# Sums of probabilities for the softmax denominator: two of four heads go from VectorE to GpSimd

## The chip, the cores and the metric

The kernel runs on one core of a Trainium2 chip. The metric is the device time of one launch in microseconds (us). A core has five engines that run their own queues in order and wait for each other by semaphores: TensorE (PE, matmuls), VectorE (DVE), ScalarE (ACT), GpSimd (POOL) and SyncE (SP, which here issues all later DMAs).

## The reference

The input has 8 sequences of 1024 rows and 512 columns. One transformer layer is computed in float32: layer norm, attention with 16 heads from latent projections and rotary embedding, a residual, layer norm, a gated FFN whose operands are rounded blockwise to an FP4 grid, a residual.

```python
scores = jnp.einsum('bhqd,bhkd->bhqk', Q, K)
scores = jnp.clip(scores, -80.0, 80.0)
scores = jnp.where(causal, scores, -jnp.inf)
weights = jax.nn.softmax(scores / jnp.sqrt(jnp.float32(d_qk)), axis=-1)
attn = jnp.einsum('bhqk,bhkd->bhqd', weights, V)
...
gate = fp4_linear(x, w_gate)
y = fp4_linear(x, w_up)
h = jax.nn.silu(gate) * y
return fp4_linear(h, w_down)
```

The change touches the softmax's denominator: the sum of the probabilities over all keys, for each query and head.

## The kernel before

The work is cut into 16 units `u` of 512 rows, two to a sequence. Attention of a unit runs over 4 groups `hq` of four heads, and in a group over blocks `j` of 128 keys: 3 steps in an even unit (the first half of a sequence, whose last step takes two narrow blocks), 7 in an odd one. That makes 320 steps. Scores are computed with the keys on the partitions, so a probability tile `pT` is 128 keys x 4 heads x 512 queries, and the denominator is a sum over partitions and over steps.

One step (`score_step`, from L589 on): TensorE computes the scores of the four heads into the one score bank `sc_ps`; ScalarE takes the exp in two halves of two heads each into `pT` (L629); VectorE clips the first half (L645), GpSimd clips the second (L648). In masked steps GpSimd also zeroes the triangle, first of the second half, then of the first (L653). `weigh`, the second part of a step, is put off until the scores of the next step are issued (`flush(1)`): TensorE multiplies `pT` with the values into the bank `num`.

The denominator has two ways. In units 1 and 3 TensorE multiplies every `pT` with ones. In all others ("summed") the first `pT` of a group is kept as accumulator, and VectorE adds each later `pT` to it (L680), two heads an instruction; a last step has four adds, of two widths. After a group's last step `divide` lets TensorE multiply the accumulator with ones (bank `den`), and `normalise` turns, inverts and multiplies on VectorE (L737 to L740).

`pT` has three buffers. One holds the accumulator until `divide`, which runs in step 1 of the next group, and the weights `wo` of the output projection take one for a while; the others alternate. An exp can therefore start only when the `pT` of two steps before is released by its readers and adders.

Between the steps TensorE's queue is filled with other pieces: the next unit's projections, the output projection (`out_proj`, L814 on VectorE), and the FFN of rows finished earlier: `gate` (copied out by ScalarE, L141, silu L893), `up` (multiplied on VectorE from PSUM, L907), `down` (L943). In units 0 to 3 the weights are quantised in place of the FFN. Three PSUM banks `ps_t` serve all these pieces. VectorE rounds the activations to the FP4 grid in chains of short instructions on the tiles `h`, `y`, `wraw` and `m` (L226 to L280). Small statistics of the layer norm run on GpSimd (L346 to L352), and ScalarE applies them (L360).

The order of every engine's queue is fixed when the program is built. A planner (`Clock`) keeps an estimated time for each of TensorE, VectorE and ScalarE. VectorE's instructions are of two kinds: urgent ones go through `on_dve(cost, ready, run)`, which first lays spare instructions that fit before `ready`; spare ones wait in two lists (`slack`) with a cost and a time from which they may run. The adds of L680 are spare ones of the first list; `need(key)` lays what is left of them before a buffer is reused or a sum is read. GpSimd is not planned.

## Time and profile before

| what | value |
|---|---|
| median of 3 runs | 3518.63 us (3517.95 to 3518.91) |
| the profiled execution's own time | 3518.86 us |
| its span, first to last instruction | 3517.1 us |
| ScalarE, exp of a half tile (L629) | 640 instructions, 566.3 us |
| GpSimd, clip (L648) | 320 instructions, 337.7 us |
| GpSimd, masks (L653) | 384 instructions, 231.3 us |
| VectorE, clip (L645) | 320 instructions, 229.3 us |

A profile is one execution. Busy times are unions of an engine's instructions; a wait is the idle time of an engine just before an instruction, put down to the instruction that ended it. A group of instructions is told as line, engine, operation, tiles written and read, shapes, count, then busy time and mean length in ns, then the idle time before them. In waits, the engine and line that waited stands first, then who was waited for. The timeline gives start, length, engine, line and operation.

### The profile page before, as it was taken

How to read it: one execution, taken by the hardware profiler on the slowest of the kernel's cores; microseconds unless marked ns; L12 is line 12 of the kernel's file. 1: busy time of each engine (PE TensorE's matmuls, PEld its weight loads, DVE VectorE, ACT ScalarE, POOL GpSimd, SP SyncE). 2: the span in 40 equal slices, each digit the busy share in tenths (PEclk: the TensorE clock that was granted, in tenths of full speed). 3: DMA queues.
4: the chain of work that ended last, by engine and by line, in shares of the span. 5: the costliest groups of instructions: out<-in, count | busy, mean ns of one | idle time of the engine just before them, and what ended most of it. 6: DMA issues, size and time to landing. Idle time of an engine off the chain costs nothing. (4 is left out here: it accounts for less than half of the span.)

```text
span 3517.1 us, 101866 instructions
## 1 busy us (share of the span) xinstructions
PE 3440.5 (98%) x45428; PEld 1526.8 (43%) x45428; DVE 2923.4 (83%) x5308; ACT 1326.2 (38%) x1850; POOL 769.0 (22%) x1086
## 2 busy tenths in 40 slices
PE   8999999999999999999999999999999999999999
PEld 3333344444444444444444444444444444444444
DVE  6878759789977889887989778899778988699887
ACT  4444443434333343333343333434343333333211
POOL 3333322112121221221221212212212222111100
PEclk9999999999999999999999999999999999999999
DMA  3212111111021101121110211111211111100110
GB/s 98 70 49 71 47 36 52 50 36 30 20 64 32 55 26 32 35 59 50 32 32 20 67 29 54 30 32 32 61 49 32 32 32 49 50 20 20 56 32 17
DMA packets 190066, 148.46 MB, mean 42 GB/s; under 512 B 126524, under 2 KB 128060, under 8 KB 189628
## 3 DMA queue, kind: packets, MB, share of 16 engines
q1 hardware_dynamic: 187780, 141.09, 13.5%
q8 instruction: 356, 5.83, 0.7%
q10 hardware_dynamic: 1848, 0.87, 0.1%
q14 instruction: 82, 0.67, 0.1%
HBM read 94.72 MB, written 33.55 MB: 36 GB/s over the span
## 5 line engine op out<-in xcount | busy, mean ns | idle before, releaser
L629 ACT ACTIVATE pT<-sc_ps 128x1024 f32<-128x1024 f32 (+1 forms) x640 | 566.3, 937 | 1069.4 <-PE sc_ps L122 835.8
L648 POOL TENSOR_SCALAR pT<-pT 128x1024 f32<-128x1024 f32 (+1 forms) x320 | 337.7, 1055 | 2325.4 <-ACT pT L629 2247.0
L122 PE MATMUL pg<-yT,wu_T 128*32 128x256 f32 x11264 | 638.5, 380 | 0.0
L122 PE MATMUL pg<-yT,wg_T 128*32 128x256 f32 x11264 | 634.5, 379 | 1.7 <-ACT yT L859 0.8
L122 PE MATMUL pd<-wd_T,h 128*32 128x512 f32 x5632 | 616.8, 592 | 2.9 <-DVE h L236 2.9
L122 PEld LDWEIGHTS pg<-yT,wg_T 128*32 128x32 f32 x11264 | 366.2, 110 | 276.9 <-issue 37.2
L680 DVE TENSOR_TENSOR pT<-pT 128x1024 f32<-128x1024 f32 (+3 forms) x528 | 459.8, 898 | 25.3 <-POOL pT L653 21.7
L122 PEld LDWEIGHTS pg<-yT,wu_T 128*32 128x32 f32 x11264 | 360.0, 110 | 264.6 <-issue 33.5
L645 DVE TENSOR_SCALAR pT<-pT 128x1024 f32<-128x1024 f32 (+1 forms) x320 | 229.3, 716 | 195.8 <-ACT pT L629 194.7
L122 PEld LDWEIGHTS pd<-wd_T,h 128*32 128x32 f32 x5632 | 182.3, 110 | 415.8 <-issue 389.8
L122 PE MATMUL sc_ps<-qc,kT 32*128 32x512 f32 (+3 forms) x3072 | 338.3, 525 | 10.8 <-ACT pT L629 10.8
L141 ACT COPY h<-pg 128x512 f32<-128x512 f32 x192 | 105.5, 550 | 629.6 <-PE pg L122 629.6
L122 PE MATMUL num<-pT,v 128*32 128x512 f32 (+3 forms) x3072 | 314.0, 496 | 17.4 <-POOL pT L653 16.9
L122 PE MATMUL sc_ps<-qr,kr 32*128 32x512 f32 (+3 forms) x3072 | 306.3, 483 | 6.9 <-DVE qr L564 6.7
L280 DVE TENSOR_TENSOR h<-h,m 128x512 f32<-128x512 f32 (+1 forms) x384 | 259.6, 676 | 10.1
L236 DVE STREAM_TRANSPOSE h<-h 128x512 f32<-128x512 f32 (+1 forms) x384 | 249.9, 658 | 4.9
L653 POOL TENSOR_SCALAR_AFFINE_SELECT pT<-pT 128x256 f32<-128x256 f32 (+1 forms) x384 | 231.3, 622 | 25.2 <-DVE pT L645 10.7
L122 PE MATMUL po<-wo,aT 128*32 128x512 f32 x2048 | 225.1, 596 | 9.1 <-DMA wo<-in_w_o_dram 4.5
L907 DVE TENSOR_TENSOR h<-pg,h 128x512 f32<-128x512 f32 x192 | 122.9, 640 | 118.5 <-PE pg L122 110.6
L122 PEld LDWEIGHTS sc_ps<-qc,kT 32*128 32x128 f32 x3072 | 114.3, 183 | 208.7 <-issue 149.8
L122 PEld LDWEIGHTS sc_ps<-qr,kr 32*128 32x128 f32 x3072 | 144.0, 185 | 114.1 <-issue 77.8
L122 PEld LDWEIGHTS num<-pT,v 128*32 128x32 f32 x3072 | 64.5, 108 | 220.8 <-issue 119.0
(97 smaller groups left out, 3528.5 us busy)
## 6 DMA issues: line engine op xcount, KB each, us to landing
xo<-in_x_dram SPq DMA_DIRECT2D x64, 256.0 KB, 2.7
wo<-in_w_o_dram SPq DMA_DIRECT2D x16, 1024.0 KB, 5.2
mid<-xo SPq DMA_DIRECT2D x64, 256.0 KB, 2.8
y<-mid SPq DMA_DIRECT2D x64, 256.0 KB, 2.8
xr<-mid SPq DMA_DIRECT2D x64, 256.0 KB, 2.7
out_dram<-xr SPq DMA_DIRECT2D x64, 256.0 KB, 2.0
xp<-in_x_dram SPq DMA_DIRECT2D x30, 512.0 KB, 3.8
xnT<-xp SPq DMA_DIRECT2D x416, 32.0 KB, 2.0
```

The lines of the kernel that those rows point to most:

```text
L122: nc.tensor.matmul(dst, **kw)
L141: on_act(0.1 + 0.0009 * src.free_size(), lambda: nc.scalar.copy(dst, src))
L236: 0.06 + 0.0013 * part.shape[1], lambda: nc.vector.transpose(part, part), key
L280: nc.vector.tensor_tensor(part, part, got["m"], op)
L629: lambda: nc.scalar.activation(part, sc[:, 2 * k : 2 * k + 2, :cols], AF.Exp, scale=SM_SCALE),
L645: lambda: nc.vector.tensor_scalar(part, part, E_HI, E_LO, ALU.min, ALU.max),
L648: nc.gpsimd.tensor_scalar(part, part, E_HI, E_LO, ALU.min, ALU.max)
L653: nc.gpsimd.affine_select(out=diag, in_=diag, pattern=[[0, 2], [0, len(segs)], [1, P]], compare_op=ALU.is_ge, fill=0.0, base=0, channel_mu ...
L680: lambda a=whole, b=part: nc.vector.tensor_tensor(a, a, b, ALU.add),
L907: lambda: nc.vector.tensor_tensor(h, pg, h, ALU.mult),
```

## The change

GpSimd adds up the probabilities of heads 2 and 3 of a group, the half that it clips itself; VectorE adds only heads 0 and 1. GpSimd's adds are issued in `weigh`, so in GpSimd's queue they stand behind the next step's clip and masks. One instruction covers two heads, as before. The planner gets a time for GpSimd (`pool`) with costs for the clip, the masks and the adds, and a table `summed` of the times at which GpSimd's adds are over; a reused `pT` and the sum of `divide` wait for them in the plan. The time `ready`, from which a step's spare adds and `weigh` are planned, is now taken from the planned ends of VectorE's and GpSimd's work.

```diff
     class Clock:
-        pe = dve = act = silu = 0.0
+        pe = dve = act = pool = silu = 0.0
         shape = None
         soon, later = deque(), deque()
-        done = {}
+        done, summed = {}, {}
...
+    def on_pool(cost, ready, run):
+        clk.pool = max(clk.pool, ready) + cost
+        run()
...
             clk.need(old, pe=False)
-            clk.act = max(clk.act, clk.done.get(old, 0.0))
+            clk.act = max(clk.act, clk.done.get(old, 0.0), clk.summed.get(old, 0.0))
             del live[old]
...
             else:
-                nc.gpsimd.tensor_scalar(part, part, E_HI, E_LO, ALU.min, ALU.max)
+                on_pool(
+                    0.08 + 0.00096 * wide,
+                    ready + 0.2,
+                    lambda: nc.gpsimd.tensor_scalar(part, part, E_HI, E_LO, ALU.min, ALU.max),
+                )
...
         while masks:
-            masks.pop()()
-        ready = clk.act + 0.4 + 0.0009 * wide + (0.7 if masked else 0.0)
+            on_pool(0.5 if len(segs) == 1 else 0.72, clk.dve, masks.pop())
+        ready = max(clk.dve, clk.pool) + 0.2
...
-            for half in halves:
+            for half in halves[:1]:
                 for _, off, at in segs:
                     whole, part = acc[0][:, half, off:], pT[:, half, at : at + U - off]
...
+            for _, off, at in segs if summed and j > 0 else ():
+                whole, part = acc[0][:, 2:4, off:], pT[:, 2:4, at : at + U - off]
+                on_pool(
+                    0.1 + 0.0044 * (U - off),
+                    ready,
+                    lambda: nc.gpsimd.tensor_tensor(whole, whole, part, ALU.add),
+                )
+                clk.summed[key] = clk.summed["sum", u, hq, 0] = clk.pool + 0.2
             live[key] = j > 0 or not summed
...
         def divide():
             clk.need(key)
+            clk.pe = max(clk.pe, clk.summed["sum", u, hq, 0])
             den = bank("den")
```

## The prediction

> **What bounds the kernel now.** I read the page first, then TensorE's waits for all 3517 us and for the part after 440 us, then VectorE and GpSimd by shape, then the timeline, and last the order of instructions that the changed source builds.

> From the page of the kernel before:

> ```profile
> span 3517.1 us, 101866 instructions
> PE 3440.5 (98%) x45428; PEld 1526.8 (43%) x45428; DVE 2923.4 (83%) x5308; ACT 1326.2 (38%) x1850; POOL 769.0 (22%) x1086
> L680 DVE TENSOR_TENSOR pT<-pT 128x1024 f32<-128x1024 f32 (+3 forms) x528 | 459.8, 898 | 25.3 <-POOL pT L653 21.7
> ```

> TensorE (PE) is busy for 3440.5 us of 3517.1; about 77 us is everything that a change to other engines can give back, 2.2%. VectorE (DVE) is the second engine with 83%, GpSimd (POOL) has 78% free. The third line is the work that the change splits: 528 adds, 459.8 us.

> TensorE's waits after 440 us (columns: total us, times, longest):

> ```profile
> PE sc_ps L122 <- ACT pT L629: 6.1, 9, 1.1
> PE num L122 <- POOL pT L653: 5.9, 10, 1.1
> PE sc_ps L122 <- DVE qr L564: 5.0, 6, 1.4
> PE pv L122 <- DVE h L907: 4.8, 3, 1.6
> PE pf L122 <- ACT kT L141: 3.9, 3, 1.3
> PE pd L122 <- DVE h L236: 2.9, 4, 0.9
> ```

> The list is short and its numbers small. All rows of this view released by VectorE or GpSimd sum to 22.3 us in 30 waits; the same sum for the first 440 us is 20.6 us in 20 waits (without the 6.3 us at the very start). So even a VectorE that is never late gives back at most 43 us. The adds themselves are nearly absent from TensorE's waits: the relief lies on an engine that is mostly not waited for.

> **What the change does to the order.** In the program built from the changed source TensorE's and ScalarE's instructions stand in the same order, one for one; SP differs in three swaps of neighbouring DMAs. VectorE has 264 adds fewer and its queue is reordered, GpSimd has 264 adds more. Each stands behind the next step's clip and masks (L648, L653), so no mask of the next step waits for it. The adds wait for GpSimd's own earlier work, which stands ahead anyway; three of them name TensorE too, whose reading is long past. New is one wait: an exp (L629) writes a probability tile that now also has to be released by GpSimd's add.

> **VectorE's side, removed.** By shape, the 528 adds are 192 of 1024 columns at 1219 ns, and 112 each of 768, 512 and 256 at 962, 733 and 451 ns. Half of each goes: 96 x 1.219 + 56 x (0.962 + 0.733 + 0.451) = 237 us.

> **GpSimd's side, added.** The trace has no wide two-input add on GpSimd. The nearest row is its clip of the same tile, one input: those clips that no VectorE instruction overlaps took 1.04 us for 1024 columns and 0.83 for 768, so 0.84 ns a column over a fixed 0.18, which gives 0.61 for 512 and 0.40 for 256. Lower end for an add of 1024 columns: 1.04 us, the second input free. Upper end: two clips and a wait for a whole VectorE add of 1.22, 3.3 us. I take two clips, 2.08 us, since a second operand of the same size is read (1.65, 1.22 and 0.80 for the narrower ones). Sum: 96 x 2.08 + 56 x (1.65 + 1.22 + 0.80) = 405 us; between 203 and 728 at the ends. GpSimd would go from 769 to some 1240 us with its own delays: it is free for that.

> **What the add does to VectorE.** This decides. Two places in the timeline:

> ```profile
> 226.12 1.04 POOL L648 TENSOR_SCALAR pT<-pT 128x1024 f32<-128x1024 f32 x1 [3.19 <-ACT pT L629]
> 226.41 1.30 DVE L645 TENSOR_SCALAR pT<-pT 128x1024 f32<-128x1024 f32 x1
> ...
> 232.08 1.29 POOL L648 TENSOR_SCALAR pT<-pT 128x1024 f32<-128x1024 f32 x1 [4.91 <-DVE wraw L266]
> ...
> 232.51 1.14 DVE L277 TENSOR_SCALAR m<-m 128x512 f32<-128x512 f32 x1
> ```

> VectorE's clip starts inside GpSimd's and ends at 227.71, 0.55 us after GpSimd ends at 227.16; undisturbed it takes 0.69. The step on `m` takes 1.14 us in place of 0.43. Over the whole trace, against the median of undisturbed instructions of the same line and shape, VectorE loses 153 us and GpSimd 148 us in this way. Stretched are VectorE's instructions with two SBUF inputs and its tensor_scalars; transposes, reductions and those that read PSUM keep their time (L907: 685 ns alone, 683 overlapped). So the two engines hold each other up, and a longer GpSimd instruction holds VectorE longer. GpSimd's present work is 629 us undisturbed: VectorE loses 0.24 us for each us of it. That is the low end for the adds, since the clip often runs while VectorE is between tasks. The adds start just where VectorE is not: in the 2 us behind the masks VectorE is busy 95% of the time, 72% with the kinds that are held. High end 0.72. I take 0.55, nearer to the high end as it is measured in the very place. 405 us of adds then cost VectorE 223 us (97 to 292) against 237 saved: **net 14 us less, between 140 less and 55 more**. The offload is about a draw on the engine that it is to relieve.

> [...]

> **The new wait of the exp.** For each summed step I took from the trace the room between the end of GpSimd's masks of the next step and the start of the exp after it, in which the add must fit. The median is 7.8 us, the least -1.5; 30 of 206 rooms are too small, by 42 us in all. What stands behind the late exp on ScalarE is the copies of PSUM banks, and TensorE's next scores, which need the score bank. TensorE's next scores came 5 to 14 us after that exp's end in most of these places (FFN matmuls lie between), so it is hidden there; not in units 0 and 2, where steps follow each other within 5 us. Room and cover together leave 2.8 us on TensorE, 5.3 with adds stretched by a quarter (as masks and clips are, 1.10 to 1.38 times), 9.2 by 1.6. I take 5 us. If the FFN cover were gone, the whole 42 us would show.

> **The reordered queue.** The planner lets VectorE run spare work up to the moment at which it thinks that a PSUM reader or a clip is ready. It knows the adds' time on GpSimd (0.1 + 0.0044 us a column of one head) but not that they hold VectorE, so the freed time is filled by FFN quantisation and the urgent instruction is late by what the adds took. Adds run 405 of 3517 us, 12%; an urgent instruction that falls into one waits half of 2.08 us on average: 0.12 us on each of the 50 waits above, 6 us; up to 25 us if the lag stays until the next idle moment (0.5 us each).

> ScalarE's normalisation (L360) waits 92 us for GpSimd's small statistics now, in 25 waits; these queue behind adds too. By the same 0.12 us it is 3 us on ScalarE, hidden behind 62% idle time; I count nothing. GpSimd issues no DMA here.

> **Sum.** Made against the profiled execution's own 3518.9 us (span 3517.1 and 1.8 around it; the median of the runs is 3518.6): +5 (exp) +6 (late VectorE) and 0 for the relief: 3529.

> **Rivals.**
> *No change that shows*, 3519 within 7 us (0.2%, about what a measurement of this kernel can tell). Speaks for it: TensorE's order is untouched and 98% busy, VectorE's balance is a draw. Both small terms need only be half as large.
> *Faster*: the adds hold VectorE by only 0.24, VectorE ends 140 us lighter (79% busy), and half of the 43 us of its and GpSimd's lateness goes: 3519 - 21 = 3498. Against it: the planner spends the freed time on spare work, so the same urgent instructions see the same queue.
> *VectorE becomes the bound* in the odd units, at 3545 to 3586. From 700 to 900 us it is busy 180 of 200 us, so about 6 us are free for each group of four heads (60 us). There the adds sum to 4 x 2.08 + 1.65 + 1.22 + 0.80 = 12.0 us; at 0.72 they hold VectorE 8.6 us against 7.0 saved. From a sum of 18 us on (0.72 x 18 - 7 = 6), so with adds of 3.1 us and more, the free 6 us are used up. At the upper end the sum is 20.5 us, 1.8 us over in each of 24 groups: 42 us, and with the urgent instructions' 25 us it is 3586.
> That the adds don't move is excluded by the built order.

> **How the numbers follow.** Slower by 7 to 40 us: 0.38 (the forecast), VectorE the bound: 0.08, no change: 0.32, faster: 0.22. Range 3504 to 3560: it leaves out about half of the faster case below and of the bound above, and keeps the ends of the unknown costs otherwise.

> **What would show it.** GpSimd's add of 1024 columns at about 2.1 us (mean 2.3 with delays), VectorE's busy time near 2910 us in place of some 2690, VectorE's instructions on `m` and `h` longer in the mean, TensorE idle some 11 us more, most of it before 440 us at scores and `num`. Wrong would be VectorE at 2750 or less with shorter rows of waits (faster), or a VectorE above 2980 with TensorE waiting for L907 and L236 (bound).

## The result, and the profile after

The changed kernel takes 3757.5 us in the median of 4 runs (3754.3 to 3758.5), the kernel before 3518.8 (also of 4). The ratio is 1.0671, with a 95% interval of 1.0658 to 1.0684: 239 us slower. The prediction of 3529 had the sign and missed the size; its range ended at 3560.

The page of the changed kernel:

```profile
span 3755.5 us, 101919 instructions
PE 3512.3 (94%) x45428; PEld 1549.7 (41%) x45428; DVE 2983.5 (79%) x5044; ACT 1325.1 (35%) x1850; POOL 1205.2 (32%) x1350
L719 POOL TENSOR_TENSOR pT<-pT 128x1024 f32<-128x1024 f32 (+3 forms) x264 | 470.6, 1782 | 10.4
L688 DVE TENSOR_TENSOR pT<-pT 128x1024 f32<-128x1024 f32 (+3 forms) x264 | 294.4, 1115 | 18.6 <-POOL pT L661 16.8
```

VectorE has 264 adds fewer and is busy 60 us longer. TensorE does the same instructions in the same order, is busy 72 us longer and idle 167 us longer (239.5 against 72.9). So two things have to be explained, the idle time and the busy time.

The idle time, in TensorE's waits of the changed kernel (total us, times, longest):

```profile
PE po L122 <- DMA wo<-in_w_o_dram: 48.5, 14, 7.0
PE num L122 <- POOL pT L661: 38.6, 31, 3.4
PE sc_ps L122 <- DVE qr L568: 30.8, 13, 3.3
PE pg L122 <- DVE xr L960: 25.7, 5, 6.8
PE sc_ps L122 <- ACT pT L633: 16.1, 26, 1.7
PE pp L122 <- DVE xr L960: 13.7, 5, 3.3
PE pg L122 <- DVE h L924: 12.3, 7, 3.4
```

The first row was small before, and `xr` as a releaser is nearly new (0.2 us before). From the same view of the kernel before:

```profile
PE po L122 <- DMA wo<-in_w_o_dram: 4.5, 4, 2.3
```

All rows of this view, summed by the releaser:

| TensorE waits for | before, us | after, us |
|---|---|---|
| the load of `wo` and other DMAs | 6 | 48 |
| GpSimd | 17 | 39 |
| VectorE | 32 | 129 |
| ScalarE | 17 | 23 |

The busy time is, nearly all of it, the clock. The mean granted clock of the two profiles:

```profile
core 0: 3517.1 us, clock 0.999
core 0: 3755.5 us, clock 0.977
```

Behind the mean stand stretches in which TensorE is granted half its clock: 3 within the span before, 35 after. Half their length, "the clock's loss" below, is 4.0 us before and 85.3 after. Part of it falls into TensorE's idle time. While TensorE is busy the stretches last 6.4 us before and 140.2 after; half of that is 3.2 and 70.1 us, so 67 of the 72 us of busy time are the clock's. 167 us of idle time and 72 of busy time are the 238 us by which the span grew (rounded).

VectorE is held up as the prediction described. By the same count, the length of its instructions against the median of undisturbed ones of the same kind, it loses 431 us to GpSimd, 153 before. Of the two kinds shown, the step on `m` is one that the prediction saw stretched, and it is longer in the mean; the transpose was not stretched, and it is not longer. After (the figure behind the busy time is the mean in ns):

```profile
L281 DVE TENSOR_SCALAR m<-m 128x512 f32<-128x512 f32 x254 | 165.0, 650 | 8.7
L240 DVE STREAM_TRANSPOSE h<-h 128x512 f32<-128x512 f32 x320 | 222.8, 701 | 3.8
```

and before:

```profile
L277 DVE TENSOR_SCALAR m<-m 128x512 f32<-128x512 f32 x254 | 122.0, 480 | 8.7
L236 DVE STREAM_TRANSPOSE h<-h 128x512 f32<-128x512 f32 x320 | 222.8, 702 | 4.1
```

The late load of `wo`, in the timeline of the changed kernel:

```profile
2099.39 0.83 POOL L655 TENSOR_SCALAR pT<-pT 128x768 f32<-128x768 f32 x1 [3.51 <-ACT pT L633]
...
2100.30 1.29 POOL L661 TENSOR_SCALAR_AFFINE_SELECT pT<-pT 128x512 f32<-128x512 f32 x2
...
2101.56 2.28 POOL L719 TENSOR_TENSOR pT<-pT 128x768 f32<-128x768 f32 x1
...
2102.18 1.94 DVE L278 TENSOR_SCALAR m<-y 128x512 uint32<-128x512 uint32 x1
...
2103.86 0.38 SPq L812 DMA_DIRECT2D wo<-in_w_o_dram  x1
...
2109.15 2.79 PE L122 MATMUL po<-wo,aT 128*32 128x512 f32 x12 [4.41 <-DMA wo<-in_w_o_dram]
```

`wo` takes a probability tile's buffer. GpSimd's add of that tile stands behind the next step's clip and masks, so it begins at 2101.56 though its own step was masked by 2092.84 (the two masks start at 2092.04 and take 0.80). SP issues the load 0.02 us after the add, TensorE's first matmul with `wo` starts 5.29 us later (the profile's page gives 5.2 us for this load, in the median), and TensorE waits 4.41 us. In the same lines VectorE's step on `m`, 0.43 us undisturbed, is held for 1.94 us by the add.

### The profile page after: what moved, and what is told of

The parts are those of the page before. It is cut to its first block, busy times and chain, and to the rows that moved or that the text cites. A ratio compares the mean times of both kernels' runs of the same rounds, so it can differ in the third digit from the quotient of the medians.

```text
span 3755.5 us, 101919 instructions
## 1 busy us (share of the span) xinstructions
PE 3512.3 (94%) x45428; PEld 1549.7 (41%) x45428; DVE 2983.5 (79%) x5044; ACT 1325.1 (35%) x1850; POOL 1205.2 (32%) x1350
## 5 line engine op out<-in xcount | busy, mean ns | idle before, releaser
L122 PE MATMUL pg<-yT,wg_T 128*32 128x256 f32 x11264 | 644.8, 384 | 35.4 <-DVE xr L960 25.7
L122 PE MATMUL pg<-yT,wu_T 128*32 128x256 f32 x11264 | 642.5, 381 | 4.6 <-DVE h L924 3.4
L122 PE MATMUL pd<-wd_T,h 128*32 128x512 f32 x5632 | 621.3, 597 | 7.5 <-DVE h L924 6.8
L122 PEld LDWEIGHTS pg<-yT,wg_T 128*32 128x32 f32 x11264 | 372.2, 111 | 316.3 <-issue 59.4
L122 PEld LDWEIGHTS pg<-yT,wu_T 128*32 128x32 f32 x11264 | 362.9, 110 | 270.7 <-issue 38.1
L719 POOL TENSOR_TENSOR pT<-pT 128x1024 f32<-128x1024 f32 (+3 forms) x264 | 470.6, 1782 | 10.4
L122 PE MATMUL num<-pT,v 128*32 128x512 f32 (+3 forms) x3072 | 321.5, 507 | 45.6 <-POOL pT L661 38.6
L122 PEld LDWEIGHTS pd<-wd_T,h 128*32 128x32 f32 x5632 | 183.8, 111 | 425.5 <-issue 399.6
L122 PE MATMUL sc_ps<-qc,kT 32*128 32x512 f32 (+3 forms) x3072 | 339.6, 526 | 16.1 <-ACT pT L633 16.1
L122 PE MATMUL sc_ps<-qr,kr 32*128 32x512 f32 (+3 forms) x3072 | 312.3, 491 | 30.8 <-DVE qr L568 30.8
L141 ACT COPY h<-pg 128x512 f32<-128x512 f32 x192 | 105.5, 550 | 659.8 <-PE pg L122 659.8
L688 DVE TENSOR_TENSOR pT<-pT 128x1024 f32<-128x1024 f32 (+3 forms) x264 | 294.4, 1115 | 18.6 <-POOL pT L661 16.8
L122 PE MATMUL po<-wo,aT 128*32 128x512 f32 x2048 | 243.4, 636 | 51.8 <-DMA wo<-in_w_o_dram 48.5
L284 DVE TENSOR_TENSOR h<-h,m 128x512 f32<-128x512 f32 (+1 forms) x384 | 279.9, 729 | 10.2
L122 PEld LDWEIGHTS sc_ps<-qc,kT 32*128 32x128 f32 x3072 | 114.9, 184 | 216.4 <-issue 144.2
```

Source lines behind the costliest of these rows:

```text
L122: nc.tensor.matmul(dst, **kw)
L141: on_act(0.1 + 0.0009 * src.free_size(), lambda: nc.scalar.copy(dst, src))
L284: nc.vector.tensor_tensor(part, part, got["m"], op)
L688: lambda a=whole, b=part: nc.vector.tensor_tensor(a, a, b, ALU.add),
L719: lambda: nc.gpsimd.tensor_tensor(whole, whole, part, ALU.add),
```

## The experiments

Three theories. A: the new planner puts VectorE's urgent instructions late. B: GpSimd's adds hold VectorE. C: the adds' place, one step late, releases tiles late. All ratios are to the kernel before, measured on the same chip beside each batch (medians 3520.9, 3522.0, 3521.0 and 3521.2).

### The square of order and adds

The first run keeps the changed kernel's planner and drops GpSimd's adds; the second keeps the old planner and its order of VectorE, and lets GpSimd add at the changed kernel's place; the third drops the adds from the second. The second's edit, against the kernel before:

```diff
-            for half in halves:
+            for k, half in enumerate(halves):
...
                     slack(
                         0.08 + 0.0025 * (U - off),
-                        lambda a=whole, b=part: nc.vector.tensor_tensor(a, a, b, ALU.add),
+                        (lambda: None)
+                        if k
+                        else lambda a=whole, b=part: nc.vector.tensor_tensor(a, a, b, ALU.add),
...
+            for _, off, at in segs if summed and j > 0 else ():
+                whole, part = acc[0][:, 2:4, off:], pT[:, 2:4, at : at + U - off]
+                nc.gpsimd.tensor_tensor(whole, whole, part, ALU.add)
             live[key] = j > 0 or not summed
```

> The changed kernel with the same order of VectorE's queue, but GpSimd issues none of its adds (left out: the later key blocks of heads 2 and 3 in the denominators). Theory A, the new planner's order of VectorE makes urgent instructions late: still above 3680. Theory B, GpSimd's adds hold VectorE up (it lost 431 us to GpSimd in place of 153): 3500 to 3540, VectorE busy near 2700. Theory C, the adds stand so late in GpSimd's queue that probability tiles come free late (exp waits 174 us for L719, wo lands late): also 3500 to 3540, and the waits for wo below 10 us.

Measured: 3500.6 us, ratio 0.9944 (0.9929 to 0.9958).

> The planner and VectorE's order of the kernel before, only without the 264 adds of the second half; GpSimd adds them at the same place as in the changed kernel, behind the next step's clip and masks. Theory A: 3520 to 3570. Theories B and C: 3680 to 3760, since the adds, their length and their place are those of the changed kernel.

Measured: 3684.9 us, ratio 1.0465 (1.0450 to 1.0481).

> As the run with the old order, but nobody adds the second half (left out: the later key blocks of heads 2 and 3 in the denominators). It completes the square of order and adds and shows what the relief of VectorE by 237 us is worth alone: 3490 to 3520 by every theory; if it is below 3500 the relief is worth more than I priced.

Measured: 3490.0 us, ratio 0.9912 (0.9896 to 0.9929).

| VectorE's order | no adds of the second half | GpSimd's adds, one step late |
|---|---|---|
| the old one | 3490 | 3685 |
| the new one | 3501 | 3757 |

The adds cost 195 us in the old order and 257 in the new one: without them the kernel is not slower in either order, so A alone is refuted. The new order costs 11 us without them and 72 with them, so it makes them dearer. The relief of VectorE alone is worth 31 us (3521 to 3490), which I had counted as nothing. TensorE's and ScalarE's instructions stand in one order in all four runs.

### The place of the add

> The old order of VectorE, and GpSimd's add stands right behind the clip and masks of its own step, ahead of the next step's clip. Theory C: at least 80 us faster than the run with the old order and the adds one step later, waits for wo below 10 us. Theory B: within 30 us of that run, since the adds hold VectorE as long. Theory A: 3520 to 3570 for both.

Measured: 4010.8 us, and it decides nothing. In step 1 the add changes the first tile of a group before TensorE has read it, so the attention of heads 2 and 3 is computed from the sum of two steps' probabilities. TensorE's order differs too, and TensorE waits for the add:

```profile
PE num L122 <- POOL pT L690: 277.6, 56, 6.7
```

The next two runs put the add behind TensorE's reading of the step before, still one step earlier than the changed kernel:

```diff
     def flush(n):
         while len(pending) > n:
             pending.popleft()()
+        while behind:
+            behind.popleft()()
...
+        def pool_adds():
+            for _, off, at in segs if summed and j > 0 else ():
+                whole, part = acc[0][:, 2:4, off:], pT[:, 2:4, at : at + U - off]
+                nc.gpsimd.tensor_tensor(whole, whole, part, ALU.add)
+
+        behind.append(pool_adds)
```

> Old order of VectorE; GpSimd's add stands behind the clip and masks of its own step and behind TensorE's reading of the step before, so one step earlier than in the changed kernel, where each sum is still right. Its length is the same. Measured so far with the adds one step later: 3685. Late release of the tiles (theory C): TensorE's 45 us of waits for wo fall below 10, with the clock's share 60 to 90 us off, 3595 to 3625. VectorE held up (theory B) alone: within 30 us of 3685.

Measured: 3598.9 us, ratio 1.0219 (1.0204 to 1.0234).

> The changed kernel's planner, and GpSimd's add one step earlier in its queue, as in the run with the old order. Measured for the changed kernel: 3757. Theory C: 60 to 90 us off, 3665 to 3700. Theory B alone: within 30 us of 3757.

Measured: 3650.5 us, ratio 1.0363 (1.0347 to 1.0378).

86 and 107 us come back, in the new order somewhat more than C expected. VectorE still loses 440 us. What is left, 109 us above the run without adds, I put down to B. The `wo` row falls in the old order, and in most of the other rows of the early run VectorE is the releaser, each time with little (the first line is of the run with late adds, the rest of the run with early adds):

```profile
PE po L122 <- DMA wo<-in_w_o_dram: 45.5, 13, 7.1
PE po L122 <- DMA wo<-in_w_o_dram: 3.5, 3, 1.9
PE num L122 <- POOL pT L655: 24.3, 29, 4.5
PE sc_ps L122 <- DVE qr L564: 20.2, 12, 3.0
PE pg L122 <- DVE h L918: 15.6, 10, 3.4
PE pd L122 <- DVE h L236: 14.2, 10, 2.5
```

To see which late release costs, one run leaves the adds late except those of step 1 of a unit's first group, whose tile `wo` takes:

```diff
-        behind.append(pool_adds)
+        early = hq == 0 and j == 1
+        if early:
+            behind.append(pool_adds)
...
+            if not early:
+                pool_adds()
             live[key] = j > 0 or not summed
```

> Old order of VectorE, adds one step late as in the changed kernel, except those of step 1 of a unit's first group, whose tile the weights wo take next: these stand in their own step. Measured: 3685 with all adds late, 3599 with all early. If the late wo is what the late place costs: 3600 to 3625 and the waits for wo below 10 us. If it is the exps that wait for a tile: 3660 to 3690.

Measured: 3616.6 us, ratio 1.0271 (1.0254 to 1.0288); the waits for `wo` are 5.4 us. Of the 86 us of the late place in the old order 68 go with the load of `wo`, 18 with all other late tiles, the exps' among them.

### The hold

GpSimd writes zeros over the part that it would have read, in the old order and at the late place:

```diff
-                whole, part = acc[0][:, 2:4, off:], pT[:, 2:4, at : at + U - off]
-                nc.gpsimd.tensor_tensor(whole, whole, part, ALU.add)
+                part = pT[:, 2:4, at : at + U - off]
+                nc.gpsimd.memset(part, 0.0)
+                nc.gpsimd.memset(part, 0.0)
+                nc.gpsimd.memset(part[:, 0], 0.0)
```

> Old order of VectorE; in place of each GpSimd add, and at its place one step late, GpSimd writes zeros over the part of the tile that it would have read, three times, for about the time of an add (left out: the later key blocks of heads 2 and 3 in the denominators). It holds the tile as long as the add but reads nothing. Theory B: VectorE's loss to GpSimd falls from 441 us to near 150 and the time to 3500 to 3570, with the waits for wo remaining. Theory C: within 50 us of 3685, since the tiles come free as late.

Measured: 3603.8 us, ratio 1.0232 (1.0215 to 1.0249): between the two expectations, so B and C each hold in part. GpSimd is busy 1182.9 us against 1215.3 with the adds, yet VectorE loses 180 us against 441. TensorE waits for `wo` as before the edit:

```profile
PE po L122 <- DMA wo<-in_w_o_dram: 53.0, 14, 7.2
PE num L122 <- POOL pT L653: 20.2, 25, 2.6
PE sc_ps L122 <- ACT pT L629: 15.9, 23, 1.7
```

The rows of `qr`, `pg` and `pd` are gone or small, the row of `wo` is not. With reads in place of writes the kernel is 81 us slower.

The trace tells the kinds apart. 384 of VectorE's instructions with two inputs overlap a memset and no other work of GpSimd: they lose nothing against undisturbed ones (-0.5 us in all). In the run with adds 158 of them overlap an add alone and lose 189 us. For these it is GpSimd's reading that holds, not its being busy. VectorE's tensor_scalars, with one input, are held by the writes too: 128 that overlap memsets alone lose 34 us, 58 that overlap adds alone 76 us.

The order in which the two costs are taken changes their sizes: late writes cost 114 us over the run without adds, and reading 81 more; early adds cost 109, and the late place 86 more. So the hold is worth some 80 to 110 us and the lateness some 85 to 115, and a single figure for each is not shown.

Then each add is cut into up to four:

```diff
-                whole, part = acc[0][:, 2:4, off:], pT[:, 2:4, at : at + U - off]
-                nc.gpsimd.tensor_tensor(whole, whole, part, ALU.add)
+                for h in (2, 3):
+                    for c in range(off, U, 256):
+                        d = min(U, c + 256)
+                        whole, part = acc[0][:, h, c:d], pT[:, h, at + c - off : at + d - off]
+                        nc.gpsimd.tensor_tensor(whole, whole, part, ALU.add)
```

> Old order of VectorE; each GpSimd add is cut into pieces of one head and at most 256 columns, up to four for one. If an add holds VectorE for its whole length and the length of a single hold matters, VectorE's urgent instructions get in between: below 3685, 3600 to 3660. If only the sum of the held time matters, the pieces' fixed cost makes it worse: 3690 to 3800.

Measured: 3682.3 us, ratio 1.0452 (1.0437 to 1.0468), as with whole adds. VectorE's loss falls to 333 us, so it does get in between; GpSimd's adds grow from 480 to 692 us, and TensorE waits longer for `wo` (64.6 us in place of 45.5). Less is lost by VectorE and more by `wo`, and the time stays, which is neither expectation.

### The clock

Of the 43 gaps above 2 us in TensorE's work after the change, 32 have a half-rate stretch that begins within 4 us of the gap's end; of 12 between 1.5 and 2 us one has, of 50 between 0.5 and 1.5 none. To test it, TensorE gets work on constants into the waits for `wo`, with VectorE's order unchanged:

```diff
         po = bank("po")
+        for _ in range(8 if t == 0 and u > 3 else 0):
+            for c in range(4):
+                nc.tensor.matmul(
+                    po[32 * c : 32 * c + 32, :],
+                    lhsT=wdq[:, 0, 32 * c : 32 * c + 32],
+                    rhs=wuv,
+                    start=True,
+                    stop=True,
+                    skip_group_check=True,
+                )
```

> The changed kernel, with eight rounds of matmuls on constants (3.4 us at full clock, results overwritten) ahead of the first output projection of each unit from unit 4 on, where TensorE waits some 4 us for wo. VectorE's order is the same. If idle time of TensorE above 2 us halves its clock for some us, as the trace of the changed kernel suggests (32 of its 43 gaps above 2 us stand beside a half-rate stretch, 1 of 12 between 1.5 and 2 us): 3715 to 3745, though TensorE has 41 us more to do. If the clock is no consequence of the gaps: 3757 to 3775.

Measured: 3769.5 us, ratio 1.0704 (1.0688 to 1.0720). That lies in the range for a clock that is no consequence of the gaps, but both ranges were worked out for too little work: the added matmuls are 85.6 us, not the 41 of my estimate, twice the waits. The clock's loss falls from 85.3 to 61.4 us even so.

> The changed kernel with four rounds of matmuls on constants instead of eight ahead of the first output projection of each unit from unit 4 on: the run with eight showed 0.86 us a round, so they were 6.9 us long, not 3.4, and longer than the wait that they fill. Four rounds are 41 us of added work in 12 units against about 44 us of waits for wo filled. If the clock is no consequence of the gaps: 3750 to 3760. If it is: the clock's loss (85 us in the changed kernel, 61 with eight rounds) falls by some 24 us and the time is 3725 to 3742.

Measured, with four rounds: 3740.3 us (3734 to 3740), ratio 1.0619 (1.0604 to 1.0633). The added work is 44.2 us, TensorE's idle time 36.9 us less, which alone would make it 7 us slower. The clock's loss falls from 85.3 to 61.4 us, by 24, and the time is 17 us shorter. More work, less time: gaps such as these waits for `wo` (4.41 us in the lines above) do cost clock.

### VectorE clips both halves

If a reading GpSimd is dear, its clip might be better on VectorE. Against the kernel before:

```diff
-            if k == 0:
+            if k < 2:
                 on_dve(
```

> The kernel before, but VectorE clips both halves, so that GpSimd keeps the masks and statistics alone. VectorE gets 204 us more (192 at 0.69 and 128 at 0.56); it is freed of being held by 306 us of GpSimd's clips. At the 0.24 us a us that I saw in the trace of before, VectorE ends 130 us heavier: 3525 to 3560. At 0.6 as the adds showed, a draw: 3500 to 3525.

Measured: 3546.0 us, ratio 1.0070 (1.0055 to 1.0085). VectorE's loss falls by 121 us, from 153 to 32, for 306 us of clips, so 0.40 us a us; its busy time is 3001.8 us, 78 more and not 130. The clips weigh more than the freedom. The time lies in the range that went with 0.24, though neither 0.24 nor 0.6 was the figure. None of the runs that compute the whole sum beats the kernel before.

## Why the prediction was wrong

The forecast was +11 us, 5 for late exps and 6 for a late VectorE; +239 were measured. The step that failed is the price of lateness on TensorE: the 6 us were too small by far, the wait for `wo` and the clock were put at nothing. The measured 3757 can be written as a path of runs: 3490 without the adds, +109 for the adds in an early place, +68 for the late `wo`, +18 for other late tiles, +72 for the new order. The prediction's steps, one by one:

- **Relief, 237 us off VectorE, worth 0.** By the lengths of the instructions 237 us is right (half of 474). In busy time, where overlapping instructions count once, VectorE has 217 us less in the run without adds and the old order. The worth was 31 us.
- **The add's length, 2.08 us for 1024 columns.** Undisturbed 2.38 us, 2.47 in the mean; 471 us in all against 405, within the bounds.
- **The hold, 0.55 us a us, VectorE 14 us lighter.** Measured 278 us more lost for 471 us, 0.59; VectorE is 60 us heavier. That the adds hold VectorE was right and the size of the hold nearly so. The two stretched rows that the prediction prints (L645 and the step on `m`) are tensor_scalars with one input, so they do not show the hold on two-input instructions; the runs with adds and with memsets do (189 us against -0.5). The loss did not reach the whole length of the adds (278 of 471 us).
- **What the lateness costs TensorE: 0.12 us on each of 50 waits, 6 us.** This term failed most. I let urgent instructions arrive at random over the whole span and let TensorE pay each delay once. The run with early adds prices it at 109 us, or 78 with the 31 us of relief taken off. Waits that were small before grew as much as the larger ones (in that run `pd` for L236 from 2.9 to 14.2 us, `pg` for the multiply from PSUM from 0.8 to 15.6), so the list of 50 was the wrong thing to multiply; even the upper price of 25 us was too low. Why the delays add up so was not taken apart further.
- **The new wait of the exp, 5 us.** The exps do wait (ScalarE 173.5 us for L719, 36 times), and little of it reaches TensorE: at most 18 us in the old order. But I looked only at exps. The same buffer is also taken by `wo`, whose load takes 5.2 us, and TensorE waits for it: 68 us. I had written that SP's order hardly changes; that was so, and the wait of its one DMA was not looked at.
- **The reordered queue, up to 25 us with the above.** 72 us on top of late adds, 52 on early ones, 11 without. A place where it shows is the multiply-out of `down`: TensorE's `pd` ended at 1977.2 us and VectorE took it from PSUM at 1988.1, behind a chain of FFN steps; TensorE then waited 6.78 us for the bank. With early adds TensorE's waits for that instruction (`xr`) are 29.6 us in the new order and 1.3 us in the old one. Which of the planner's new terms does it was not separated; that is open.
- **TensorE's clock was left out.** I treated its 3440 us as fixed. 67 of the 239 us are lost clock, on top of the 167 us of idle time.
- **The rival with VectorE as the bound** did not happen either: VectorE is idle 21% of the span. The sign that the prediction gave for it, a VectorE above 2980 us, did come (2983.5). What failed is not its throughput but its punctuality.

## What to carry to other kernels

GpSimd was idle for 78% of the span before, and adds moved to it still held VectorE: price such work in the donor's held time (here 0.59 us for each us of GpSimd's adds), not in the helper's idle time. When an instruction moves in a queue, list everybody who waits for the buffers that it releases, loads above all, since a load's own latency then comes on top (5.2 us for `wo`, in the median). Where TensorE is 98% busy, price a new gap of some us with the clock that it costs (here 67 us of busy time in all), and look for punctuality, not for shares of busy time.
